# A graph layer on one core: a fill between gathers, a lighter first part, a look-up summed in PSUM and packing operands in PSUM

## The chip, the core and the metric

The kernel runs on one core of a Trainium2 chip. The core has a matrix engine (PE, which writes PSUM), a vector engine (DVE), an activation engine (ACT), a general engine (POOL) and a DMA-issuing engine (SP), each with its own queue of instructions that runs in order; they meet through semaphores. Times are device microseconds of one launch, from the first instruction to the last; lower is better. The time before is 3158.25 us, the median of 3 runs (3149.09 to 3170.76).

## What is computed

One layer for N = 6250 nodes with D = 256 features and 206,250 directed edges (`src`, `dst`). Its first half sums two branches over the layer-normalised input; its second half is a mixture of 8 experts with the two best per node.

```
xn = layernorm(x)
# branch 1: graph attention, 4 heads (gnn)
h = xn @ W                        # 64 features
el, er = h @ Wl.T, h @ Wr.T       # 4 scores each
e = exp(leaky_relu(el[src] + er[dst], 0.2))
w = e / rowsum(e over edges of src)
out_h = elu(segment_sum(w_h * h[dst], src) + b)     # 4 x 64
# branch 2: linear attention over all nodes, 4 heads of 32 (mix), with rmsnorms
q, k, v = split(rmsnorm(xn) @ w_qkv)
k = softmax over the nodes;  context = k v^T;  out = rmsnorm(q context @ w_out + b) + xn
x = x + branch1 + branch2
# experts
t = layernorm(x); top 2 of 8 by router
x = x + t + sum_e combine_e * (gelu(t @ w1_e + b1_e) @ w2_e + b2_e)
```

## The kernel before

Nodes are cut into 49 tiles of 128 (`NT`), edges into 1612 columns of 128 (`EC`).

**First part.** `project(t0, n)` takes four node tiles at a time: it loads x, takes the statistics, normalises (`xn`, L310, on DVE), transposes on PE, multiplies by one joined weight matrix and copies the parts of the PSUM result away: q, k and v with a scale, the row of `table` that the edges gather (4 scores, 64 features and a one, `tab`), and `el`. A running maximum of k (`kmax`) goes along. After each project() three calls of `sort_batch` follow, each over 32 columns of edges: a one-hot of the source's pair of tiles (`ob`, L365), counts on PE (`n_ps`), a scan (`inc`), the number of edges ahead (`before`, L380), ranks through two matmuls (`r_ps`, with the triangular matrix `tri` and `ones16`), and a matmul that puts each edge into its cell of `grid`. Then `context()` subtracts the maximum from k (L468, on DVE), takes Exp and sums k v^T.

**Middle.** A loop runs over the 49 node tiles. For each tile b there are 35 columns of 128 edges. `pack(q)` orders the edges of the pair of tiles 2q and 2q+1: one-hots `ohc` (L858) and `ohp` (L870), products `rc` (L865), matmuls into `s_ps` (L875), and from it the indices `dst_x` (L884, clamped in L886). `gather` then issues 35 indirect DMAs on POOL per tile (L906), each of 128 rows of `table`, into tiles `xe` of 7 columns, of which there are 8: a tile needs five, so the gathers can run 1.6 tiles ahead at most. `look(b, k)` fetches el of each edge's source: one-hots `oh` (L919), transposes, matmuls `e_ps` (L939) in two halves, each with a reduce into `er` (L943). `weights` lines up `er` with the edge columns (`z`, L960 to L964), adds the gathered scores (five adds `z<-z,xe`, L967, one for each xe tile), takes the leaky maximum and Exp (`ew`) and copies it to PSUM (`ew_s`, L972). `sums(k)`, k = 0 to 3, weighs the one-hots (`ohw`, L980) and accumulates 45 matmuls into `a_ps` (L987); it is the last reader of xe.

Between the four steps of a tile stand pieces of other work: `look(b + 1, k)`, at k = 1 of every even tile `pack` of the next pair, and one piece of the second branch's attention or of the experts (`finish_steps`: h_ps L731, Gelu into hT L739, y_ps L747, x L751). The order in which each engine gets its instructions is made by the framework's scheduler when the program is built; each engine then keeps to it. POOL's queue in this part holds the gathers alone. A gather waits for the indices, for a free xe and for the gather eight before it.

The PSUM tile `bank` holds `ew_s` and the bias row `gb_s`. At the end a flag tells whether some pair had more edges than fit; only then a slow path runs.

Of the kernel before, what the change touches and what calls it, by code (L numbers as in the profile page):

```python
# [8 lines left out]
F32 = mybir.dt.float32  # L9
# [8 lines left out]
P = 128  # L18
# [17 lines left out]
def tile_gps_layer(  # L36
# [174 lines left out]
    tri = sp.tile([P, P], F16, name="tri")  # L211
    nc.vector.tensor_scalar(tri, iota_f, piota, None, op0=OP.is_gt)
# [3 lines left out]
    starts = sp.tile([NB, BW // CB, CB], F32, name="starts")  # L216
    nc.vector.memset(starts, 1.0)
    nc.vector.memset(starts[:, :, 0:1], 0.0)
# [69 lines left out]
    def project(t0, n):  # L288
# [16 lines left out]
        tab = qw.tile([P, GT, TW], F32, name="tab")  # L305
        nc.gpsimd.memset(tab[:, :, TW - 1:TW], 1.0)  # L306
        for j in range(n):
            t = t0 + j
            xn = qw.tile([P, D], F32, name="xn")
            nc.vector.tensor_scalar(  # L310
                xn, xt[:, j, :], stats[:, t, 0:1], rstd[:, t:t + 1],
                op0=OP.subtract, op1=OP.mult,
            )
            xT_ps = mps.tile([P, DC, P], F32, name="tp")
            for c in range(DC):
                nc.tensor.transpose(xT_ps[:, c, :], xn[:, c * P:(c + 1) * P], ident)
            xT = qw.tile([P, DC, P], F32, name="xT")
            nc.scalar.copy(xT, xT_ps)
            pr = mps.tile([P, PW], F32, name="pr")
            for c in range(DC):  # L320
                nc.tensor.matmul(
                    pr, lhsT=xT[:, c, :], rhs=wcat[:, c, :], start=(c == 0), stop=(c == DC - 1)
                )
            nc.scalar.activation(q_all[:, t, :], pr[:, :HID], AF.Copy, scale=rn[:, j:j + 1])
            nc.scalar.activation(
                kv[:, t, :2 * HID], pr[:, HID:3 * HID], AF.Copy, scale=rn[:, j:j + 1]
            )
            nc.scalar.copy(tab[:, j, :TW - 1], pr[:, O_TAB:O_EL])
            nc.vector.tensor_copy(el[:, t, :], pr[:, O_EL:PW])
            rows = P if t < NT - 1 else last  # L330
            k_t = kv[:rows, t, :HID]
            if t == 0:
                nc.vector.tensor_copy(kmax, k_t)
            else:
                nc.vector.tensor_max(kmax[:rows], kmax[:rows], k_t)
        nc.sync.dma_start(
            out=table[t0 * P:(t0 + n) * P, :].rearrange("(t p) f -> p t f", p=P),
            in_=tab[:, :n, :],
# [9 lines left out]
    def sort_batch(t):  # L348
# [20 lines left out]
        n_ps = sps.tile([NB, BW], F32, name="n_ps")  # L369
        for c in range(w):  # L370
            nc.tensor.matmul(
                n_ps[:, c:c + 1], lhsT=ob[:, c, :], rhs=ones16[:, 0:1], start=True, stop=True
            )
        inc = sw.tile([NB, BW], F32, name="inc")
        nc.vector.tensor_tensor_scan(
            inc[:, :w], flat(starts)[:, :w], n_ps[:, :w], 0.0,
            op0=OP.mult, op1=OP.add,
        )
        before = sw.tile([NB, BW, 2], F16, name="before")
        nc.vector.tensor_tensor(  # L380
            before[:, :w], inc[:, :w, None].to_broadcast([NB, w, 2]),
            n_ps[:, :w, None].to_broadcast([NB, w, 2]), op=OP.subtract,
        )
        if w == BW:
            nc.scalar.copy(ntot[:, bs], inc[:NQ].rearrange("q (b c) -> q b c", c=CB)[:, :, CB - 1])
        else:
            for b, e in enumerate(ends):
                nc.scalar.copy(ntot[:, bs][:, b:b + 1], inc[:NQ, e - 1:e])
        ahead = sw.tile([NB, BW, NB], F16, name="ahead", bufs=1)
        nc.vector.tensor_tensor(  # L390
            pairs(ahead[:, :w]), two(before[:, :w], NB // 2), row(delta, NB // 2), op=OP.mult
# [3 lines left out]
        for i, a in enumerate(range(0, w, BB)):  # L395
            z = min(w, a + BB)
            part = r_ps[:, i, :(z - a) * NB]
            nc.tensor.matmul(part, lhsT=tri, rhs=flat(ob[:, a:z]), start=True, stop=False)
            nc.tensor.matmul(
                part, lhsT=ones16[:NB, :], rhs=flat(ahead[:, a:z]), start=False, stop=True  # L400
            )
# [9 lines left out]
        rank = sw.tile([P, BW], F16, name="rank")  # L411
        with nc.allow_low_precision("one summand of each sum is not zero"):
            nc.vector.tensor_reduce(rank[:, :w], r16[:, :w], axis=AX.X, op=OP.add)
        rank2 = sw.tile([P, BW, 2], F16, name="rank2")
        nc.vector.tensor_copy(rank2[:, :w], rank[:, :w, None].to_broadcast([P, w, 2]))
# [25 lines left out]
    def context():  # L441
        km_ps = mps.tile([HID, P], F32, name="tp")
# [23 lines left out]
        for t0, n in groups:  # L466
            kk = kv[:, t0:t0 + n, :HID]
            nc.vector.tensor_sub(kk, kk, krow[:, None, :].to_broadcast([P, n, HID]))  # L468
# [333 lines left out]
    yps = gx.enter_context(tc.tile_pool(name="yp", bufs=2, space=PSUM))  # L802

# [3 lines left out]
    gb_s = bank[:, 512 - FO:]  # L807
# [7 lines left out]
    def pack(q):  # L815
# [8 lines left out]
        for u in range(U):  # L824
# [6 lines left out]
            total = pe.tile([P, S, NBT], F32, name="e_ps")  # L831
# [21 lines left out]
        iota_2 = pairs(iota_h)[:, None]  # L853
        s_ps = pl.tile([P, 2, U * CW], F32, name="s_ps")
        for t0 in range(0, NBT, PB):
# [8 lines left out]
            for i in range(2):  # L864
                nc.vector.tensor_tensor(  # L865
                    pairs(rc[:, :m, i, :]), pairs(ohc[:, :m]),
                    twos(grid[:, q, t0:t0 + m, i, :], U * CW // 2), op=OP.mult,
# [31 lines left out]

    def gather(dst_x):  # L900
        xes = []
        for k in range(CPT // EB):
            xe = gw.tile([P, EB, TW], F32, name="xe", bufs=8)
            for j in range(EB):
                c = k * EB + j
                nc.gpsimd.indirect_dma_start(  # L906
# [4 lines left out]
                )  # L911
# [3 lines left out]
    def look(b, k):  # L915

        if k == 0:
# [3 lines left out]
                pairs(iota_b[:, :SN])[:, None].to_broadcast([P, GC * S, SN // 2, 2]),  # L921
# [3 lines left out]
            seen[b] = oh, gw.tile([P, GC, S, H], F32, name="er")  # L925
        elif k < 3:
            oh, er = seen[b]
# [9 lines left out]
            e_ps = pe.tile([P, gh, S, 3, H], F32, name="e_ps")  # L937
            for g in range(gh):
                nc.tensor.matmul(  # L939
                    e_ps[:, g].rearrange("p s i h -> p (s i h)"), lhsT=ohT[:, g, :],  # L940
                    rhs=elw[:, b].rearrange("p s i h -> p (s i h)"), start=True, stop=True,
                )
            nc.vector.tensor_reduce(  # L943
                er[:, g0:g0 + gh].rearrange("p g s h -> p (g s) h"),
                e_ps.rearrange("p g s i h -> p (g s) h i"), axis=AX.X, op=OP.add,
            )

    def weights(xes, er):
        z = gw.tile([P, CW, H], F32, name="z")

        def of(q0, n, a, m):

            zq = z[:, q0 * CS:(q0 + n) * CS].rearrange("p (s j) h -> p s j h", j=CS)
            return zq[:, :, a:a + m]

        def er_of(q0, n, a, m):
            return er[:, a:a + m, q0:q0 + n].rearrange("p g s h -> p s g h")

        more = GC - 1 - CS
        nc.vector.tensor_copy(of(0, S, 0, CS), er_of(0, S, 1, CS))  # L960
        nc.vector.tensor_copy(z[:, CPT - more:CPT], er[:, GC - more:, S - 1])
        head, tail = of(1, S - 1, 0, more), of(0, S - 1, CS - 1, 1)
        nc.vector.tensor_add(head, head, er_of(0, S - 1, GC - more, more))
        nc.vector.tensor_add(tail, tail, er_of(1, S - 1, 0, 1))  # L964
# [3 lines left out]
        zz = z[:, :CPT]  # L968
        nc.vector.scalar_tensor_tensor(zz, zz, 0.2, zz, op0=OP.mult, op1=OP.max)
        ew = gw.tile([P, CPT, H], F32, name="ew")  # L970
        nc.scalar.activation(ew, zz, AF.Exp)
# [40 lines left out]
    for t0, n in blocks:  # L1012
        x2 = gw.tile([P, GT, D], F32, name="x2", bufs=3)
        for j in range(n):
            b = t0 + j
            xes, _ = ready.pop(b)
            oh, er = seen.pop(b)
            weights(xes, er)
# [159 lines left out]
```

## Time and profile before

| | |
|---|---|
| median of the runs | 3158.25 us (3149.09 to 3170.76, 3 runs) |
| the profiled execution | 3989.86 us, span 3988.1 us |
| granted PE clock in it, mean | 0.717 |
| gathers | 1715, 965 ns each on POOL |
| first gather starts | 491.59 us |
| DMA engines, mean | 26 GB/s moved |

The profiled execution is a fourth longer than the runs without a profile, so shares of its span are not shares of the median. Three lines to learn the page's form (instruction group, shapes, count, then busy time and mean in ns, then idle time before and what ended it):

```profile
L870 DVE TENSOR_TENSOR ohp<-to,iota_h 128x2048 f16<-128x2048 f16 x150 | 182.9, 1220 | 24.6 <-remote 16.4 <-PE s_ps L875 4.4 <-ACT to L851 3.8
L943 DVE TENSOR_REDUCE er<-e_ps 128x96 f32<-128x288 f32 x98 | 44.1, 450 | 102.5 <-PE a_ps L987 42.1 <-PE e_ps L939 30.1 <-remote 20.5
masks.py:197 POOL MEMSET ident<- 128x128 f32 x1 | 0.2, 204 | 0.3 <-POOLq L1158 0.3
```

The last one is a memset of 128 elements per partition on POOL, at the program's start.

### The profile page before, as it was taken

How to read it: one execution, taken by the hardware profiler on the slowest of the kernel's cores; microseconds unless marked ns; L12 is line 12 of the kernel's file. 1: busy time of each engine (PE TensorE's matmuls, PEld its weight loads, DVE VectorE, ACT ScalarE, POOL GpSimd, SP SyncE). 2: the span in 40 equal slices, each digit the busy share in tenths (PEclk: the TensorE clock that was granted, in tenths of full speed). 3: DMA queues.
4: the chain of work that ended last, by engine and by line, in shares of the span. 5: the costliest groups of instructions: out<-in, count | busy, mean ns of one | idle time of the engine just before them, and what ended most of it. 6: DMA issues, size and time to landing. Idle time of an engine off the chain costs nothing.

```text
span 3988.1 us, 40348 instructions
## 1 busy us (share of the span) xinstructions
PE 2343.3 (59%) x15298; PEld 1728.2 (43%) x15298; DVE 2045.5 (51%) x4719; ACT 681.1 (17%) x1365; POOL 1666.2 (42%) x1753
## 2 busy tenths in 40 slices
PE   6787633354546666656766573573674654655758
PEld 3444423333334544444544352452453443443546
DVE  8888843456445445534625543553453445255353
ACT  3333201111111211211211110110110101101113
POOL 1000076544654454463454545436345444545430
PEclk8776556666667877776868686686786776776879
DMA  1001012111211111110111101101011011111110
GB/s 57 28 21 17 13 26 45 29 38 43 46 47 48 27 19 23 21 35 14 26 19 23 25 17 26 22 14 33 16 21 28 18 23 21 21 21 25 19 20 9
DMA packets 106684, 103.98 MB, mean 26 GB/s; under 512 B 42726, under 2 KB 78788, under 8 KB 106484
## 3 DMA queue, kind: packets, MB, share of 16 engines
q0 software_dynamic: 54880, 60.70, 9.0%
q1 hardware_dynamic: 49908, 39.75, 3.5%
q8 instruction: 122, 2.00, 0.2%
q10 hardware_dynamic: 1696, 0.89, 0.1%
q14 instruction: 78, 0.64, 0.1%
HBM read 86.57 MB, written 14.65 MB: 25 GB/s over the span
## 4 chain that ended last, share of the span: by engine, by line
another core or an unknown queue 30%; PE 26%; DVE 19%; issue 5%; ACT 3%; POOL 1%; DMA 0%; DVEq 0%; ACTq 0%; POOLq 0%
PE y_ps L747 7%; PE a_ps L987 7%; PE h_ps L731 7%; DVE rc L865 4%; DVE ohp L870 4%; DVE ohc L858 2%; DVE ohw L980 2%; PE s_ps L875 1%; PE y_ps L722 1%; POOL xe L906 1%; PE y_ps L671 1%; PE t_ps L932 1%; PE y_ps L559 1%; ACT ohT L936 1%
## 5 line engine op out<-in xcount | busy, mean ns | idle before, releaser
L906 POOL DMA_INDIRECT xe<-table,dst_x x1715 | 1654.9, 965 | 1901.0 <-issue 767.3
L987 PE MATMUL a_ps<-ohw,xe 128*65 128x128 f32 x4410 | 693.8, 316 | 295.5 <-issue 171.5
L987 PEld LDWEIGHTS a_ps<-ohw,xe 128*65 128x65 f32 x4410 | 614.6, 165 | 392.3 <-issue 229.9
L980 DVE TENSOR_TENSOR ohw<-oh,bank 128x1280 f32<-128x1280 bf16 x196 | 322.6, 1649 | 631.6 <-remote 524.3
L731 PE MATMUL h_ps<-tokT,w1s 128*128 128x512 f32 (+2 forms) x896 | 438.9, 609 | 176.0 <-ACT hT L739 173.3
L747 PE MATMUL y_ps<-w2s,hT 128*128 128x256 f32 x1568 | 434.9, 420 | 73.6 <-DVE x L751 44.1
L747 PEld LDWEIGHTS y_ps<-w2s,hT 128*128 128x128 f32 x1568 | 323.5, 213 | 196.2 <-issue 94.1
L751 DVE SCALAR_TENSOR_TENSOR x<-y_ps,comb,x 128x256 f32<-128x256 f32 x392 | 186.6, 481 | 379.8 <-PE y_ps L747 198.3
L875 PE MATMUL s_ps<-rc,ohp 128*128 128x144 f16 x2525 | 241.3, 264 | 164.9 <-DVE rc L865 156.4
L875 PEld LDWEIGHTS <-ohp 128*128 128x128 f16 x2525 | 219.2, 116 | 216.8 <-issue 127.5
L731 PEld LDWEIGHTS h_ps<-tokT,w1s 128*128 128x128 f32 x896 | 166.3, 210 | 291.8 <-ACT hT L739 198.5
L739 ACT ACTIVATE hT<-h_ps,b1s 128x512 f32<-128x512 f32 (+2 forms) x224 | 142.0, 634 | 828.3 <-PE h_ps L731 379.7
L865 DVE TENSOR_TENSOR rc<-ohc,grid 128x1152 f16<-128x1152 f16 (+1 forms) x350 | 229.1, 693 | 5.2 <-remote 5.2
L870 DVE TENSOR_TENSOR ohp<-to,iota_h 128x2048 f16<-128x2048 f16 (+1 forms) x175 | 195.1, 1115 | 24.6 <-remote 16.4
L722 PE MATMUL y_ps<-b2s,cTs 8*128 8x256 f32 x98 | 53.3, 640 | 208.9 <-issue 107.9
L936 ACT COPY ohT<-t_ps 128x768 bf16<-128x768 bf16 x98 | 78.1, 797 | 334.1 <-remote 144.7
L939 PE MATMUL e_ps<-elw,ohT 128*128 128x48 bf16 x588 | 39.9, 199 | 157.5 <-ACT ohT L936 84.5
L858 DVE TENSOR_TENSOR ohc<-to,iota_h 128x1152 f16<-128x1152 f16 (+1 forms) x175 | 121.3, 694 | 8.8 <-ACT to L851 8.8
L722 PEld LDWEIGHTS y_ps<-b2s,cTs 8*128 8x128 f32 x98 | 21.9, 276 | 230.2 <-issue 122.6
L932 PE MATMUL t_ps<-identb,oh 128*128 128x128 bf16 x588 | 68.6, 269 | 86.7 <-DVE oh L919 79.0
L306 POOL MEMSET tab<- 128x4 f32 x13 | 1.3, 108 | 282.0 <-DMA table<-tab 282.0
L723 DVE TENSOR_TENSOR x<-x,y_ps 128x256 f32<-128x256 f32 x49 | 20.5, 421 | 191.6 <-remote 83.9
(261 smaller groups left out, 2748.6 us busy)
## 6 DMA issues: line engine op xcount, KB each, us to landing
xe<-table,dst_x POOLq DMA_INDIRECT x1715
xt<-in_x_dram SPq DMA_DIRECT2D x24, 512.0 KB
base_y<-xt SPq DMA_DIRECT2D x12, 512.0 KB
yt<-base_y SPq DMA_DIRECT2D x11, 512.0 KB
out_dram<-x SPq DMA_DIRECT2D x11, 512.0 KB
w1s<-in_L_ffn_w_dram SPq DMA_DIRECT2D x8, 256.0 KB
w2s<-in_L_ffn_w_dram SPq DMA_DIRECT2D x8, 256.0 KB
table<-tab SPq DMA_DIRECT2D x12, 138.0 KB
```

The source lines that it names most:

```text
L731: nc.tensor.matmul(h_ps[:, :w], lhsT=w1s[:, e, c, f * P:(f + 1) * P], rhs=held["tokT"][:, c, :w], start=(c == 0), stop=(c == DC - 1),)
L739: nc.scalar.activation(held[e][:, f, :w], h_ps[:, :w], AF.Gelu, bias=b1s[:, k:k + 1])
L747: nc.tensor.matmul(y_ps, lhsT=held[e][:, f, j * P:(j + 1) * P], rhs=w2s[:, e, f, :], start=(f == 0), stop=(f == FC - 1),)
L751: nc.vector.scalar_tensor_tensor(x2[:, j, :], y_ps, held["comb"][:, j, e:e + 1], x2[:, j, :], op0=OP.mult, op1=OP.add,)
L858: nc.vector.tensor_tensor(pairs(ohc[:, :m]), twos(to[:, 0, t0:t0 + m], U * CW // 2), iota_2[:, :, :U * CW // 2].to_broadcast([P, m, U * CW ...
L865: nc.vector.tensor_tensor(pairs(rc[:, :m, i, :]), pairs(ohc[:, :m]), twos(grid[:, q, t0:t0 + m, i, :], U * CW // 2), op=OP.mult,)
L870: nc.vector.tensor_tensor(pairs(ohp[:, :m]), twos(to[:, 1, t0:t0 + m], P // 2), iota_2.to_broadcast([P, m, P // 2, 2]), op=OP.is_equal,)
L875: nc.tensor.matmul(flat(s_ps), lhsT=ohp[:, t - t0, :], rhs=flat(rc[:, t - t0]), start=(t == 0), stop=(t == NBT - 1),)
L906: nc.gpsimd.indirect_dma_start(out=xe[:, j, :], out_offset=None, in_=table, in_offset=bass.IndirectOffsetOnAxis(ap=dst_x[:, c:c + 1], axis=0),
L936: nc.scalar.copy(ohT, t_ps)
L980: nc.vector.tensor_tensor(ohw[:, :n], oh[:, g0:g1, i, None, :].to_broadcast([P, n, H, SN]), ew_s[:, c0:c0 + n, :, None].to_broadcast([P, n ...
L987: nc.tensor.matmul(a_ps[:, i].rearrange("f h n -> f (h n)"), lhsT=xes[c // EB][:, c % EB, H:], rhs=ohw[:, c - c0].rearrange("p h n -> p (h ...
```

## The change

It has four parts.

1. In `gather`, a memset of 128x128 f32 (one of 16 slots of `pause`) stands on POOL in front of each indirect DMA, and dependencies without a semaphore fix the order memset, gather, memset, gather.
2. The first part: `xn` goes from DVE to ACT (with `shift` = -mean * rstd as bias), `el` is copied with `tab` on ACT and split off on POOL, `kmax` becomes one reduce at the start of context(), the subtraction of the maximum goes to POOL, the rank's copy to ACT. In sort_batch the count matmul gives two columns, count and zero, so that a scan over 64 elements yields the inclusive count without a `before`; where `tri` was, `upto` (minus one where column <= row) stands, and the rank's reduce is halved by a fold first.
3. The look-up: the 12 matmuls of a tile add into one PSUM tile `e_ps` by edge column, after one matmul with zeros; a single reduce in `weights` replaces two reduces and four copies and adds. `total` in pack() moves from the PSUM pool `pe` to `pt`.
4. Packing: `iota_h`, `iota_b` and the pair's slice of `grid` are copied into `bank` as f32 words and read from PSUM as 16-bit operands by ohc, ohp, rc and oh.

```
@@ project
-        tab = qw.tile([P, GT, TW], F32, name="tab")
-        nc.gpsimd.memset(tab[:, :, TW - 1:TW], 1.0)
+        shift = qw.tile([P, GT], F32, name="shift")
+        nc.vector.scalar_tensor_tensor(
+            shift[:, :n], stats[:, t0:t0 + n, 0], -1.0, rs, op0=OP.mult, op1=OP.mult
+        )
+        tab = qw.tile([P, GT, TW - 1 + H], F32, name="tab")
...
-            nc.vector.tensor_scalar(
-                xn, xt[:, j, :], stats[:, t, 0:1], rstd[:, t:t + 1],
-                op0=OP.subtract, op1=OP.mult,
+            nc.scalar.activation(
+                xn, xt[:, j, :], AF.Identity, bias=shift[:, j:j + 1], scale=rstd[:, t:t + 1]
             )
...
-            nc.scalar.copy(tab[:, j, :TW - 1], pr[:, O_TAB:O_EL])
-            nc.vector.tensor_copy(el[:, t, :], pr[:, O_EL:PW])
-            rows = P if t < NT - 1 else last
-            k_t = kv[:rows, t, :HID]
-            if t == 0:
-                nc.vector.tensor_copy(kmax, k_t)
-            else:
-                nc.vector.tensor_max(kmax[:rows], kmax[:rows], k_t)
+            nc.scalar.copy(tab[:, j, :], pr[:, O_TAB:PW])
+        nc.gpsimd.tensor_copy(el[:, t0:t0 + n, :], tab[:, :n, TW - 1:])
+        nc.gpsimd.memset(tab[:, :n, TW - 1:TW], 1.0)
@@ sort_batch
-        n_ps = sps.tile([NB, BW], F32, name="n_ps")
+        n_ps = sps.tile([NB, BW, 2], F32, name="n_ps")
         for c in range(w):
             nc.tensor.matmul(
-                n_ps[:, c:c + 1], lhsT=ob[:, c, :], rhs=ones16[:, 0:1], start=True, stop=True
-            )
-        inc = sw.tile([NB, BW], F32, name="inc")
+                n_ps[:, c, :], lhsT=ob[:, c, :], rhs=one_none, start=True, stop=True
+            )
+        inc = sw.tile([NB, BW, 2], F16, name="inc")
         nc.vector.tensor_tensor_scan(
-            inc[:, :w], flat(starts)[:, :w], n_ps[:, :w], 0.0,
-            op0=OP.mult, op1=OP.add,
-        )
-        before = sw.tile([NB, BW, 2], F16, name="before")
-        nc.vector.tensor_tensor(
-            before[:, :w], inc[:, :w, None].to_broadcast([NB, w, 2]),
-            n_ps[:, :w, None].to_broadcast([NB, w, 2]), op=OP.subtract,
+            flat(inc[:, :w]), starts.rearrange("q b c two -> q (b c two)")[:, :2 * w],
+            flat(n_ps[:, :w]), 0.0, op0=OP.mult, op1=OP.add,
         )
...
-            nc.tensor.matmul(part, lhsT=tri, rhs=flat(ob[:, a:z]), start=True, stop=False)
+            nc.tensor.matmul(part, lhsT=upto, rhs=flat(ob[:, a:z]), start=True, stop=False)
...
+        fold = NB // 4 * 2
+        nc.vector.tensor_tensor(
+            r16[:, :w, :fold], r16[:, :w, :fold], r16[:, :w, NB - fold:], op=OP.add
+        )
-            nc.vector.tensor_reduce(rank[:, :w], r16[:, :w], axis=AX.X, op=OP.add)
+            nc.vector.tensor_reduce(
+                rank[:, :w], r16[:, :w, :NB - fold], axis=AX.X, op=OP.add
+            )
-        nc.vector.tensor_copy(rank2[:, :w], rank[:, :w, None].to_broadcast([P, w, 2]))
+        nc.scalar.copy(rank2[:, :w], rank[:, :w, None].to_broadcast([P, w, 2]))
@@ context
+        nc.vector.tensor_reduce(
+            kmax, kv[:, :NT - 1, :HID].rearrange("p t d -> p d t"), axis=AX.X, op=OP.max
+        )
+        nc.vector.tensor_max(kmax[:last], kmax[:last], kv[:last, NT - 1, :HID])
...
-            nc.vector.tensor_sub(kk, kk, krow[:, None, :].to_broadcast([P, n, HID]))
+            nc.gpsimd.tensor_sub(kk, kk, krow[:, None, :].to_broadcast([P, n, HID]))
@@ middle: bank
+    none = gw.tile([1, (1 + CPT) * 3 * H], BF16, name="none", bufs=1)
+    nc.vector.memset(none, 0.0)
...
-    gb_s = bank[:, 512 - FO:]
+    gb_s = bank[:, CPT * H:CPT * H + FO]
+    words = CPT * H + FO
+    iota_p = bank[:, words:words + P // 2]
+    iota_q = bank[:, words + P // 2:words + (P + SN) // 2]
+    words += (P + SN) // 2
+    edges = bank[:, words:words + 2 * NBT]
+    nc.vector.tensor_copy(iota_p, iota_h.bitcast(F32))
+    nc.vector.tensor_copy(iota_q, iota_b[:, :SN].bitcast(F32))
+    iota_p, iota_q = iota_p.bitcast(F16), iota_q.bitcast(BF16)
@@ pack
-            total = pe.tile([P, S, NBT], F32, name="e_ps")
+            total = pt.tile([P, S, NBT], F32, name="t_ps")
...
+        nc.vector.tensor_copy(
+            edges, grid[:, q].rearrange("p t i two -> p (t i two)").bitcast(F32)
+        )
+        edges_q = edges.bitcast(F16).rearrange("p (t i two) -> p t i two", i=2, two=2)
-        iota_2 = pairs(iota_h)[:, None]
+        iota_2 = pairs(iota_p)[:, None]
...
-                    twos(grid[:, q, t0:t0 + m, i, :], U * CW // 2), op=OP.mult,
+                    twos(edges_q[:, t0:t0 + m, i, :], U * CW // 2), op=OP.mult,
@@ gather
+    rows = []
+    pause = gw.tile([P, 16, P], F32, name="pause", bufs=1)
+
+    def behind(ins, by=mybir.DependencyClass.NoSync):
+        if rows:
+            tc.add_manual_dep(
+                ins.ins, rows[-1].ins.name,
+                mybir.DependencyInfo(by, mybir.DependencyReason.DATA),
+            )
+        rows.append(ins)
...
-                nc.gpsimd.indirect_dma_start(
+                slot = len(rows) // 2 % 16
+                behind(nc.gpsimd.memset(pause[:, slot], 0.0))
+                behind(nc.gpsimd.indirect_dma_start(
...
@@ look
-            seen[b] = oh, gw.tile([P, GC, S, H], F32, name="er")
+            seen[b] = oh, pe.tile([P, 1 + CPT, 3, H], F32, name="e_ps")
...
-            e_ps = pe.tile([P, gh, S, 3, H], F32, name="e_ps")
+            if k == 1:
+                nc.tensor.matmul(
+                    e_ps.rearrange("p c i h -> p (c i h)"), lhsT=identb[0:1, :], rhs=none,
+                    start=True, stop=False,
+                )
             for g in range(gh):
                 nc.tensor.matmul(
-                    e_ps[:, g].rearrange("p s i h -> p (s i h)"), lhsT=ohT[:, g, :],
-                    rhs=elw[:, b].rearrange("p s i h -> p (s i h)"), start=True, stop=True,
-                )
-            nc.vector.tensor_reduce(
-                er[:, g0:g0 + gh].rearrange("p g s h -> p (g s) h"),
-                e_ps.rearrange("p g s i h -> p (g s) h i"), axis=AX.X, op=OP.add,
-            )
+                    e_ps[:, g0 + g::CS][:, :S].rearrange("p s i h -> p s (i h)"),
+                    lhsT=ohT[:, g, :],
+                    rhs=elw[:, b].rearrange("p s i h -> p s (i h)"),
+                    start=False, stop=(g0 + g == GC - 1),
+                )
@@ weights
-        nc.vector.tensor_copy(of(0, S, 0, CS), er_of(0, S, 1, CS))
-        nc.vector.tensor_copy(z[:, CPT - more:CPT], er[:, GC - more:, S - 1])
-        head, tail = of(1, S - 1, 0, more), of(0, S - 1, CS - 1, 1)
-        nc.vector.tensor_add(head, head, er_of(0, S - 1, GC - more, more))
-        nc.vector.tensor_add(tail, tail, er_of(1, S - 1, 0, 1))
+        nc.vector.tensor_reduce(
+            z, e_ps[:, 1:].rearrange("p c i h -> p c h i"), axis=AX.X, op=OP.add
+        )
```

## The prediction

> **What bounds the kernel now.** I read the page first: span, busy shares, slices, the head of the chain.
>
> ```profile
> span 3988.1 us, 40348 instructions
> PE 2343.3 (59%) x15298; PEld 1728.2 (43%) x15298; DVE 2045.5 (51%) x4719; ACT 681.1 (17%) x1365; POOL 1666.2 (42%) x1753
> POOL 1000076544654454463454545436345444545430
> another core or an unknown queue 30%; PE 26%; DVE 19%; issue 5%; ACT 3%; POOL 1%; DMA 0%; DVEq 0%; ACTq 0%; POOLq 0%
> L906 POOL DMA_INDIRECT xe<-table,dst_x x1715 | 1654.9, 965 | 1901.0 <-issue 767.3
> ```
>
> No engine is full. The POOL digits show three stretches: a first part without gathers, a long middle with them, a short tail. The windows give each its own numbers (columns: us, then busy time and count of PE, PEld, DVE, ACT, POOL, then granted clock, DMA share, GB/s):
>
> ```profile
> 0.00:491.00 491.00, 352.47 (x3954) 218.51 (x3954) 427.48 (x973) 153.15 (x475) 11.36 (x38) 0.72 0.11 25
> 491.00:3860.00 3369.00, 1882.36 (x10851) 1434.21 (x10851) 1571.93 (x3602) 482.46 (x808) 1654.80 (x1715) 0.71 0.13 27
> 3860.00:3988.00 128.00, 108.51 (x493) 75.50 (x493) 46.12 (x146) 45.45 (x82) 0.08 (x1) 0.88 0.05 8
> ```
>
> The first part is DVE's (427 of 491 us, 87%), the tail PE's. In the middle POOL sets the rhythm; its timeline (start, length, in brackets the idle time before and what ended it):
>
> ```profile
> 1784.76 0.94 POOL L906 DMA_INDIRECT xe<-table,dst_x  x1 [0.30 <-issue]
> 1836.39 1.65 POOL L906 DMA_INDIRECT xe<-table,dst_x  x1 [50.69 <-issue]
> ...
> 2980.01 0.95 POOL L906 DMA_INDIRECT xe<-table,dst_x  x1 [28.80 <-PE y_ps L747]
> 2981.26 0.94 POOL L906 DMA_INDIRECT xe<-table,dst_x  x1 [0.30 <-issue]
> 2982.51 0.94 POOL L906 DMA_INDIRECT xe<-table,dst_x  x1 [0.30 <-issue]
> ```
>
> In a burst a gather starts every 1.25 us (0.94 and 0.30). 1715 of them are 2139 us of the middle's 3369; in the other 1230 us POOL waits. The long waits, like the 28.80, come before every even tile: POOL wants `dst_x` of the next pair of tiles, and pack() on DVE is not done (its `dst_x` clamp, L886, began at 2979.08). Shorter ones are for xe buffers (350.6 us released by a_ps L987).
>
> Why is pack late? In a burst PE slows down: from 3000 to 3018 us it starts a matmul every 1.2 to 2.6 us, its wait put to "issue", where 0.11 us is usual at full clock; DVE waits for it.
>
> ```profile
> 3011.23 0.20 PE L939 MATMUL e_ps<-elw,ohT 128*128 128x48 bf16 x1 [1.91 <-issue]
> 3012.61 0.20 PE L939 MATMUL e_ps<-elw,ohT 128*128 128x48 bf16 x1 [1.19 <-issue]
> 3022.43 1.75 DVE L980 TENSOR_TENSOR ohw<-oh,bank 128x1536 f32<-128x1536 bf16 x1 [26.37 <-remote]
> ```
>
> First part and tail, without gathers, have no such stall. The profiled execution took 3989.86 us, the median of the runs is 3158.25: 832 us less, while the stalls are some 30% of 3988. So I take most of the stall to be the profile's own. On the median my ledger is 491 + 2139 + 128 = 2758 and some 400 us of POOL waiting, 17 us for each of the 24 pairs. That split is an estimate; no row shows the unprofiled run.
>
> **The change, part by part.**
>
> *Fill between gathers.* 1715 memsets of 128x128 f32. A memset of that size (masks.py:197, ident) took 204 ns, so 350 us on POOL's queue if nothing overlaps, 0 if it fits into the 0.30 us gap. Below nothing only if the spacing frees PE in the bursts, which I weigh as a rival. The full price stands by its row; but the 1.25 us rhythm may itself be a little slow under the profile. For both together I take the middle of 2139 and 2489: 2314 us. Each xe tile also comes 7 x 0.2 us later; z adds and a_ps wait for it.
>
> *First part.* DVE loses xn 19.7, kmax 13.3, before 9.9, rank2 9.0, kv subtract 8.0, el 7.8, tri 3.1: 70.8 us. It gains shift (13 x 0.17 = 2.2), one kmax reduce of 6144 elements (at L413's 1003 ns for 832: 7), 32 more scan elements x 50 (1.7); rank by fold and half-size reduce is 0.35 + 0.60 against 1.00 us, -2.6 in all. Net -63 us. ACT takes xn (49 x 0.42, by L562) and rank2 (50 x 0.19), +30 us on 153 of 491: covered, though DVE now waits for ACT's rank2 with only rv to do meanwhile. POOL takes the 13 kv subtracts: 0.67 us each by DVE's row, 1.3 at twice that; POOL is idle there (its waits for table stores are 282 us). The table stores now wait for POOL's el copy and memset instead of ACT; nobody waits for them before the first gather. First gather at about 441: -50, ends 0 and -63.
>
> *Look-up in PSUM.* Off DVE: 98 reduces of 450 ns (44 us) and four z operations (0.23, 0.16, 0.19, 0.17 us) x 49 (37 us). On: 49 reduces of 420 elements, 0.59 us by scaling L943 (29 us). -52 us over 49 tiles, but in front of the z adds, which wait for gathers: I take 0. PE gets 49 zero-matmuls of 432 columns (0.43 us by L832's 0.405: 21 us), covered by a PE that is 56% busy.
>
> *Packing operands in PSUM.* 25 copies of edges (0.36 us by L972: 9 us). The large question is the rate. L870 (ohp, 2048 f16 elements, both operands in SBUF) took 1220 ns, two per cycle. No row here reads f16 from PSUM. In f32 a PSUM operand costs nothing: L838 with one 568 ns, L839 without 561. The Trainium skill (VectorE: DVE Perf Modes, "The perf-mode tier table") speaks against this edit: tensor_tensor with any PSUM operand runs at one element per cycle. Its Vector Engine (DVE) Microarchitecture Reference ("5.1 Performance modes") asks for 16-bit unit-step operands but not SBUF in that mode. By the first, 34,744 elements per pack at 0.52 ns more are 18 us x 25 = 452 us, and oh 49 x 0.8 = 39; by the second nothing. I take the second and keep the first as a rival.
>
> *What moves: DVE's order.* This decides my forecast. I compared the built instruction order. Before, in 22 of the 24 packs that run inside the tile loop the five adds of gathered rows for the next tile (z<-z,xe, L967) stand behind all 14 rc multiplies. After, in 14 of 24 all five adds stand ahead of at least 12 of the 14 rc (packs 1 to 7, 10, 13, 15, 17, 19, 21, 23); in 7 more ahead of the last few operations. DVE runs in order, so there pack waits for the odd tile's last gather to land; then come ohc, ohp, rc and the index arithmetic; only then has POOL indices. Queued behind the waiting add are also ohw of k=2 and 3 (now behind all rc), so a_ps and the xe buffers it frees. Price: landing 2 us (tile 0: gathers end at 539, `ew` is copied at 543.4, between them 2.4 us of adds, Exp and its table), then from the first ohc to dst_x 23 us (2956.08 to 2979.27), two ohw 3.5, some routing operations 2: about 30 us of idle POOL per gated pair, 14 x 30 = 420 us. The trace of before has this case twice: packs 6 and 10 stand behind four and three of the adds, and POOL waited 38.0 and 50.7 us there, against 23 to 30 elsewhere late in the run. For the ten other pairs I take 5 us (50), for buffers 3 us x 24 (72).
>
> **Sum.** 441 + 2314 + 420 + 50 + 72 + tail 128 = 3425; rounded 3430, +8.6% on 3158. In a profiled execution the same edits act on 3988, where pack already ran after the bursts; there I expect a smaller change, -5% to +10%.
>
> **Rivals.**
> 1. *The bursts' stalls are real and the fill loosens them* (faster). For it: 30% of the chain. Against: PE trickles record by record, and the median lacks 832 us of it. Place: PE between 7 gathers into a burst and its end. Price: at best the 400 us of POOL waiting fall to 200 and the fill hides half: 441 + 2314 + 200 + 128 = 3083; it decides if the gated packs cost less than the 17 us per pair paid now. 13%.
> 2. *The fill hides in the gap* and only the gate remains: 2139 for 2314, 3250. 17%.
> 3. *One element per cycle from PSUM*: 18 us more in front of each dst_x, on the path in the gated pairs and half of the rest: 19 x 18 = 342, 3770. 6%.
> 4. *It cancels*: the gate binds only where POOL waits already, the first part pays for the fill: 3158 - 50 + 40, within 1%. 8%.
>
> **How the numbers follow.** My case has 56%, with 3300 to 3590 by the two ends of the fill. The range 3120 to 3590 leaves out rival 1 and rival 3. 1% is about what a measurement of this kernel can tell from no change (its three runs lie 0.7% apart). Faster 0.13; within 1% 0.08; slower 0.56 + 0.17 + 0.06 = 0.79.
>
> **What would show it.** After: the gather's period in bursts (1.25 if hidden, 1.45 if not); POOL's idle before even tiles (30 us or more in the listed pairs, released by DVE); ohp at 1220 ns or 2280; the first gather near 441; PE's "issue" trickle in bursts gone or not. I am wrong if the median falls below 3127, which means that the stalls exist outside the profile, or if the gated pairs wait no longer than the others.

## The result, and the profile after

The changed kernel takes 3508.68 us (median of 4 runs, 3507.48 to 3511.68) beside 3156.69 us for the kernel before (4 runs, 3149.09 to 3170.76): ratio 1.1111, 95% interval 1.1071 to 1.1151. It is slower by 11%, on a chip of this kind. Another kind turned up in the experiments, and there the answer has the other sign.

First the page of the changed kernel: span, engines, and the groups that answer to those shown before.

```profile
span 3506.6 us, 42107 instructions
PE 2212.4 (63%) x15347; PEld 1630.4 (46%) x15347; DVE 1992.4 (57%) x4307; ACT 722.9 (21%) x1471; POOL 2082.0 (59%) x3494
L945 POOL DMA_INDIRECT xe<-table,dst_x x1715 | 1655.0, 965 | 934.6 <-PE a_ps L1016 621.6
L944 POOL MEMSET pause<- 128x128 f32 x1715 | 382.5, 223 | 60.5 <-PE g_ps L433 59.5
L997 DVE TENSOR_TENSOR z<-z,xe 128x28 f32<-128x28 f32 x245 | 44.4, 191 | 845.4 <-DMA xe<-table,dst_x 801.7
L895 DVE TENSOR_TENSOR ohp<-to,bank 128x2048 f16<-128x2048 f16 (+1 forms) x175 | 194.9, 1114 | 0.0
```

No engine is full. POOL is idle for 934.6 us in front of its gathers (some 285 of it is the usual gap of 0.17 us; the ledger below has the real waits), and DVE waits 801.7 us in its adds of gathered rows for those same gathers: the two wait for each other in turn. ohp reads f16 from PSUM at 1114 ns in the mean.

The three stretches of the run, cut some 20 us before the first gather and 4 us before the last one (columns as in the prediction):

```profile
0.00:434.00 434.00, 326.77 (x3869) 198.43 (x3869) 380.46 (x756) 190.56 (x580) 48.72 (x65) 0.76 0.13 29
434.00:3380.00 2946.00, 1782.55 (x11003) 1360.35 (x11004) 1566.84 (x3415) 487.04 (x812) 2029.22 (x3423) 0.74 0.15 31
3380.00:3507.00 127.00, 103.04 (x477) 71.60 (x475) 45.05 (x139) 45.30 (x79) 4.11 (x7) 0.88 0.07 9
```

Now one gated pack, on DVE's timeline (start, length, engine and line, then in brackets the idle time before), and POOL's first gather after it:

```profile
1273.27 0.19 DVE L997 TENSOR_TENSOR z<-z,xe 128x28 f32<-128x28 f32 x1 [1.67 <-DMA xe<-table,dst_x]
1273.37 0.26 DVE L867 TENSOR_TENSOR to_i<-inc 128x101 int32<-128x101 f32 x1
1283.04 0.19 DVE L997 TENSOR_TENSOR z<-z,xe 128x28 f32<-128x28 f32 x1 [9.41 <-DMA xe<-table,dst_x]
...
1283.42 0.20 DVE L868 TENSOR_SCALAR to_i<-to_i 128x101 int32<-128x101 int32 x1
...
1284.16 0.75 DVE L883 TENSOR_TENSOR ohc<-to,bank 128x1152 f16<-128x1152 f16 x1
...
1309.43 0.20 DVE L911 TENSOR_SCALAR dst_x<-dst_x 128x72 int32<-128x72 int32 x1
```

```profile
1310.37 0.95 POOL L945 DMA_INDIRECT xe<-table,dst_x  x1 [29.72 <-PE a_ps L1016]
1311.32 0.22 POOL L944 MEMSET pause<- 128x128 f32 x1
```

The fifth add stands in the queue between two steps of pack's index arithmetic. It waits 9.41 us, until tile 13's last rows have landed; only then come all of ohc, rc and ohp, and dst_x 26 us later. POOL starts 0.7 us after dst_x, after 29.72 us of idling. The trace names a_ps as what ended that wait, because the wait is for several semaphores; what came last is the dst_x clamp, whose end lies directly before the gather.

From POOL's timeline I made one ledger for every kernel. *First*: start of gather 0. *Rhythm*: the time from the first to the last gather without the waits. *Waits*: idle time of POOL beyond the usual gap, in front of even tiles (where a new pair begins) and elsewhere. *Tail*: from the last gather to the end. "Stalls" marks runs on chips on which the kernel before takes some 3960 us (see below).

| kernel, us | first | rhythm | waits, even tiles | other waits | tail | span |
|---|---|---|---|---|---|---|
| changed | 455 | 2310 | 607 | 12 | 122 | 3507 |
| e1 no fill | 455 | 2165 | 618 | 13 | 127 | 3379 |
| e2 pack first | 455 | 2317 | 321 | 5 | 129 | 3227 |
| e3 operands in SBUF | 452 | 2396 | 251 | 11 | 128 | 3237 |
| e4 before + fill | 494 | 2394 | 185 | 9 | 128 | 3210 |
| e7 before, stalls | 491 | 2181 | 681 | 487 | 128 | 3967 |
| e5 before + first part, stalls | 453 | 2181 | 641 | 495 | 127 | 3898 |
| e6 no fill, pack first, stalls | 453 | 2158 | 811 | 373 | 128 | 3923 |
| e10 changed, stalls | 457 | 2308 | 737 | 215 | 133 | 3850 |
| e9 fill, pack earlier, stalls | 455 | 2310 | 29 | 897 | 129 | 3820 |

### The profile page after: what moved, and what is told of

The parts are those of the page before. It is cut to its first block, busy times and chain, and to the rows that moved or that the text cites. A ratio compares the mean times of both kernels' runs of the same rounds, so it can differ in the third digit from the quotient of the medians.

```text
span 3506.6 us, 42107 instructions
## 1 busy us (share of the span) xinstructions
PE 2212.4 (63%) x15347; PEld 1630.4 (46%) x15347; DVE 1992.4 (57%) x4307; ACT 722.9 (21%) x1471; POOL 2082.0 (59%) x3494
## 5 line engine op out<-in xcount | busy, mean ns | idle before, releaser
L945 POOL DMA_INDIRECT xe<-table,dst_x x1715 | 1655.0, 965 | 934.6 <-PE a_ps L1016 621.6
L1016 PE MATMUL a_ps<-ohw,xe 128*65 128x128 f32 x4410 | 611.5, 299 | 298.5 <-issue 230.1
L1016 PEld LDWEIGHTS a_ps<-ohw,xe 128*65 128x65 f32 x4410 | 563.2, 155 | 338.0 <-issue 245.9
L997 DVE TENSOR_TENSOR z<-z,xe 128x28 f32<-128x28 f32 x245 | 44.4, 191 | 845.4 <-DMA xe<-table,dst_x 801.7
L756 PE MATMUL y_ps<-w2s,hT 128*128 128x256 f32 x1568 | 405.2, 395 | 127.4 <-DVE x L760 107.0
L944 POOL MEMSET pause<- 128x128 f32 x1715 | 382.5, 223 | 60.5 <-PE g_ps L433 59.5
L890 DVE TENSOR_TENSOR rc<-ohc,bank 128x1152 f16<-128x1152 f16 (+1 forms) x350 | 227.6, 692 | 1.9 <-DVE z L997 0.2
L895 DVE TENSOR_TENSOR ohp<-to,bank 128x2048 f16<-128x2048 f16 (+1 forms) x175 | 194.9, 1114 | 0.0
L883 DVE TENSOR_TENSOR ohc<-to,bank 128x1152 f16<-128x1152 f16 (+1 forms) x175 | 121.1, 692 | 0.0
L427 DVE TENSOR_TENSOR ohp<-rank,iota_h 128x4096 f16<-128x4096 f16 (+1 forms) x51 | 115.7, 2270 | 2.8 <-ACT rank L420 2.8
L325 PE MATMUL pr<-wcat,xT 128*128 128x456 f32 x196 | 106.3, 670 | 5.8 <-ACT xT L322 4.3
```

The costliest lines, as they stand in the source:

```text
L756: nc.tensor.matmul(y_ps, lhsT=held[e][:, f, j * P:(j + 1) * P], rhs=w2s[:, e, f, :], start=(f == 0), stop=(f == FC - 1),)
L883: nc.vector.tensor_tensor(pairs(ohc[:, :m]), twos(to[:, 0, t0:t0 + m], U * CW // 2), iota_2[:, :, :U * CW // 2].to_broadcast([P, m, U * CW ...
L890: nc.vector.tensor_tensor(pairs(rc[:, :m, i, :]), pairs(ohc[:, :m]), twos(edges_q[:, t0:t0 + m, i, :], U * CW // 2), op=OP.mult,)
L895: nc.vector.tensor_tensor(pairs(ohp[:, :m]), twos(to[:, 1, t0:t0 + m], P // 2), iota_2.to_broadcast([P, m, P // 2, 2]), op=OP.is_equal,)
L944: behind(nc.gpsimd.memset(pause[:, slot], 0.0))
L945: behind(nc.gpsimd.indirect_dma_start(out=xe[:, j, :], out_offset=None, in_=table, in_offset=bass.IndirectOffsetOnAxis(ap=dst_x[:, c:c + 1 ...
```

## The experiments

### On the chip without stalls

**e1, no fill.**

```
-                behind(nc.gpsimd.memset(pause[:, slot], 0.0))
```

> The changed kernel without the 1715 memsets; 12 instead of 14 packs stand behind the next tile's adds. My theory now (the fill's net price is 0.09 us a gather; a gated pair pays it on 70 gathers, a free pair only on the 35 of its even tile, because its pack is late anyhow): 14 x 6.3 + 10 x 3.2 = 120 us less, 3390 us. The prediction's own term (2314 for 2139) says 175 less, 3333. Rival, the fill is the whole slowdown: about 3157 - 37 = 3120. For the profile: if the fill alone takes the profile's inflation away, this kernel's profiled execution is again some hundreds of us above its median, with matmuls 1.2 us and more apart in the bursts.

Measured: 3381.65 us (3380.26 to 3383.16), 1.0734 [1.07, 1.0768] of before (3152.42 on this chip, 0.1% from the 3156.69 beside the changed kernel). The fill costs 127 us in this order; theory 120. The rhythm falls by 145 us, 0.085 us for each gather: of a memset's 0.223 us the rest fits into the gap. Of the 145 us, 12 come back as longer waits and 5 in the tail. The whole slowdown is not the fill's: 229 us are left. The last sentence of the expectation failed: without the fill, the profiled execution is still as long as the others (3381.0).

**e2, pack first.** The adds of gathered rows get an order-only dependency on the last dst_x clamp.

```
-        nc.vector.tensor_scalar_min(dst_x, dst_x, NPAD - 1)
+        packed.append(nc.vector.tensor_scalar_min(dst_x, dst_x, NPAD - 1))
...
-            nc.vector.tensor_add(zk, zk, xe[:, :, :H])
+            add = nc.vector.tensor_add(zk, zk, xe[:, :, :H])
+            tc.add_manual_dep(
+                add.ins, packed[-1].ins.name,
+                mybir.DependencyInfo(
+                    mybir.DependencyClass.NoSync, mybir.DependencyReason.DATA
+                ),
+            )
```

> The changed kernel, with the adds of gathered rows ordered behind the dst_x clamp of the last pack, so that no pack is gated; fill and all else stay. By the prediction's prices (30 us for a gated pair, 5 for a free one) 14 x 25 = 350 us less: 3160. By the waits in the changed kernel's own trace (28 to 32 us for a gated pair, 18 to 20 for a free one) only 14 x 11 = 154 less: 3355, with 18 us of POOL idle before every even tile. Rival, the order costs nothing: 3508.

Measured: 3229.98 us (3228.59 to 3235.84), 1.0258 [1.0224, 1.0292]. The order alone is worth 279 us, more than any other part of the change. In the ledger all of it is the wait before even tiles, 607 to 321. By pairs, the 14 listed in the prediction fall from 29.1 us each (25.2 to 32.0) to 9.7; the other ten from 20.0 to 18.6. Both my numbers were off: 350 by the prediction's prices, 154 by "28 to 32 against 18 to 20". One of the ten, pair 8, waits 29.6 us although no add stands ahead of its pack; the other nine wait 17.7 to 20.1. A gated pair without its gate does not fall to the level of the others, but below, because its pack starts earlier: pair 7's first ohc comes 3.7 us after the odd tile's last gather in the changed kernel, and 8.5 us before it in e2.

**e3, operands in SBUF.**

```
-        iota_2 = pairs(iota_p)[:, None]
+        iota_2 = pairs(iota_h)[:, None]
...
-                    twos(edges_q[:, t0:t0 + m, i, :], U * CW // 2), op=OP.mult,
+                    twos(grid[:, q, t0:t0 + m, i, :], U * CW // 2), op=OP.mult,
...
-                pairs(iota_q)[:, None].to_broadcast([P, GC * S, SN // 2, 2]),
+                pairs(iota_b[:, :SN])[:, None].to_broadcast([P, GC * S, SN // 2, 2]),
```

> The changed kernel with iota_h, iota_b and grid read from SBUF as before, no copies into bank. The built order has then 3 gated packs for 14. Theory (the PSUM operands cost nothing in themselves, they only changed the scheduler's order): as the run with pack first, 11 x 11 = 120 less, 3390; by the prediction's prices 11 x 25 = 275 less, 3233. Rival, operands in PSUM gain time or cost it by themselves: this run and the one with pack first lie more than 60 us apart.

Measured: 3235.46 us (3234.17 to 3238.84), 1.0268 [1.0235, 1.03]: 5 us from the run with pack first. So it is this part of the change, the operands in PSUM with the copies into `bank` that go with them, that led the scheduler to the gating order (how it did was not looked into); undone alone, with fill, first part and look-up kept, it gives back 273 of the 279 us. But "they cost nothing in themselves" hides two effects that cancel. The gathers take 1014 ns in the mean here and 969 with operands in PSUM, and the rhythm is 2396 for 2317: the PSUM operands make POOL 79 us faster. First this run's kind of gather beside pack, in the kernel before with fill (e4), where the operands are also in SBUF; then the same stretch of work with operands in PSUM (e2):

```profile
1305.33 0.22 POOL L919 MEMSET pause<- 128x128 f32 x1
1305.72 0.95 POOL L920 DMA_INDIRECT xe<-table,dst_x  x1 [0.17 <-issue]
1306.67 0.22 POOL L919 MEMSET pause<- 128x128 f32 x1
1307.05 1.42 POOL L920 DMA_INDIRECT xe<-table,dst_x  x1 [0.17 <-issue]
```

```profile
1260.18 0.95 POOL L947 DMA_INDIRECT xe<-table,dst_x  x1 [0.17 <-issue]
1261.13 0.22 POOL L946 MEMSET pause<- 128x128 f32 x1
1261.52 0.95 POOL L947 DMA_INDIRECT xe<-table,dst_x  x1 [0.17 <-issue]
```

While ohc, ohp and rc run, gathers of 0.95 us become 1.42 us in the first and not in the second; over all 1715, 166 are longer than 1.3 us in e4 and 28 in e2. In the mean, gathers that lie beside ohp take 1343 ns in e4 (116 of them) and 951 in e2 (79), beside rc 1262 and 956, beside ohc only 1030 and 951; beside ohw, which has one operand in PSUM in both kernels, 957 and 954. So the instruction beside a gather makes the difference, and not the kernel as a whole. The DVE instructions themselves keep their times (rc 692 ns in e3, 689 in e2). The Trainium skill (SBUF — State Buffer, "Who interferes with whom") says that a DVE instruction with two SBUF inputs contends with a GpSimd instruction that reads SBUF, and one with at most one SBUF input, outside the modes that use both ports, does not; these rows agree.

**e4, the kernel before with the fill alone** (the memset and its order, as in the change).

> The kernel before with the fill and its fixed order alone; the order on DVE is that of before (no pack gated). Theory: 24 free pairs x 35 gathers x 0.09 = 77 us more, 3235. The prediction's term: 175 more, 3332. Rival, the fill hides in the gap: 3157. Profile: if the stalls of the kernel before are the profile's own and come from gathers issued without a pause, this kernel's profiled execution lies within 1% of its median and its burst matmuls are no longer 1.2 us apart.

Measured: 3213.08 us (3211.55 to 3214.78), 1.02 [1.0167, 1.0232], so 61 us more; theory 77. Here, where no pack is gated, most of the fill's 145 us seems to be paid out of waits that POOL would have had anyway; the kernel before has no trace without stalls that could show them. In the ledger 11 of the 24 pairs wait less than 3 us; in eight of these pack's first scan runs ahead of the copy of the even tile's `ew_s`.

### On chips with stalls

**e5, e6, e7, e8** ran on another chip. There the kernel before takes 3965.72 us (median of 19 runs, all but one of them between 3940.8 and 3985.36), 813 us more than on the first. The totals expected of e5, e6 and e8 were meant for a chip without stalls; here only the difference from the kernel before can be read.

> The kernel before, nothing changed, profiled once more. If its profiled execution is always long (3990 us, matmuls 1.2 us and more apart in bursts), it is again above 3900. If that was one odd execution, this one lies within 1% of 3152, and its trace shows what the median run does: about 17 us of POOL idle before each even tile by the prediction's ledger (400 us in 24 pairs).

e7 is the kernel before, unchanged: its profiled execution takes 3968.97 us, as long as the other runs on its chip. One group of its page, ohw on DVE, against the same group of e1 (the last numbers are DVE's idle time before it, and what ended most of that; "remote" is a release to which the trace shows no instruction):

```profile
L980 DVE TENSOR_TENSOR ohw<-oh,bank 128x1280 f32<-128x1280 bf16 x196 | 322.5, 1649 | 608.0 <-remote 454.9
```

```profile
L1006 DVE TENSOR_TENSOR ohw<-oh,bank 128x1280 f32<-128x1280 bf16 x196 | 323.0, 1648 | 78.0 <-PE a_ps L1013 75.9
```

And matmuls of a_ps within a burst, PE's timeline, first e7, then e1 (x20 are 20 matmuls in a row):

```profile
2427.14 0.37 PE L987 MATMUL a_ps<-ohw,xe 128*65 128x128 f32 x1 [0.98 <-issue]
2428.55 0.37 PE L987 MATMUL a_ps<-ohw,xe 128*65 128x128 f32 x1 [1.04 <-issue]
2431.34 0.37 PE L987 MATMUL a_ps<-ohw,xe 128*65 128x128 f32 x1 [2.42 <-issue]
```

```profile
629.80 2.35 PE L1013 MATMUL a_ps<-ohw,xe 128*65 128x128 f32 x20
```

POOL gathers at the same pace in both (1.27 and 1.26 us each), but in e7 PE starts one matmul in 1.4 to 2.8 us, and in e1 twenty in 2.35 us. The stall does not come from the profiler, since the profiled executions of e1 to e4 have none and are as short as their other runs. It goes with the chip; each chip was used in one session only, so that chip and session cannot be told apart. The long "remote" idle time before ohw is also in the 3990 us execution shown before the change (524.3 us): that one was most likely taken on such a chip, while the 3158 us median came from the other kind. A lower granted clock does not explain the stall. Before the first gather the clock is 0.72 in e7 and 0.71 in e4 (the kernel before with the fill, no stalls), and the first gather comes at 491 and 494 us; within bursts it is 0.58 and 0.78, a quarter less, while PE's rate in the table under e10 falls to less than a quarter (0.89 for 4.04).

**e5, first part alone** (the kernel before with the new project, sort_batch and context).

> The kernel before with the lighter first part alone (the middle and its order as before, but one more pack, the fourth, behind two adds). The first gather starts 37 us earlier (455 for 492), one more gated pair costs 11: 3152 - 37 + 11 = 3126. The prediction's term: 3152 - 50 = 3102. Rival, the first part's gain is lost again in the middle: 3152.

Measured 3917.18 us (14 runs), 0.9904 [0.9868, 0.9939]. In the ledger the first gather comes 38 us earlier (453 for 491), and the gain is kept.

**e6, no fill and pack first** (both edits of e1 and e2).

> The changed kernel without the fill and with no pack gated: first part, look-up in PSUM and operands in PSUM are what is left of the change. Theory (gate and fill are the whole loss): the free pairs of the run with pack first pay the fill on the 35 gathers of the even tile alone, 24 x 3.2 = 77 less than its 3230: 3153. If all 70 gathers of a pair count, 154 less: 3076. Rival, look-up and PSUM operands cost time of their own on the path: above 3170.

Measured 3923.5 us, 0.9909 [0.9874, 0.9945]. What it takes on a chip without stalls was not seen. Here nothing beyond what the first part's 38 us explain comes through.

**e8, pack one tile earlier, no fill.** The gathers leave pack() and stay where they were.

```
+    packed = {}
+
+    def fetch(q):
+        for b in range(q * U, min(q * U + U, NT)):
+            idx, loc = packed.pop(b)
+            ready[b] = (gather(idx), loc)
...
-                if k == 1 and b % U == 0 and b + U < NT:
-                    pack(b // U + 1)
+                if k == 1 and b % U == 0 and b + U < NT:
+                    fetch(b // U + 1)
+                if k == 1 and b % U == 1 and b + U + 1 < NT:
+                    pack(b // U + 2)
```

> The changed kernel without the fill, pack of a pair one tile earlier (in the odd tile before the pair's predecessor ends), gathers where they were; no pack is gated. Theory (the chain from the even tile's last gather to dst_x, some 60 us against the odd tile's 44 us of gathers, is what POOL waits for in every pair): POOL no longer waits for indices, only for buffers; 455 + 2139 + 122 = 2716 at the least, with 100 us of buffer waits 2820. Rival, buffers (a_ps behind ohw) or PE end the wait at the same place: 3100 and above.

Measured 4027.78 us, 1.0187 [1.0151, 1.0223]. The wait before even tiles is gone (77 us), but 1209 us appear elsewhere, before odd tiles and inside tiles. PE starts 0.68 matmuls a us in bursts and 4.06 in POOL's pauses. My reading, which no run isolates, is that PE's work needs those pauses, wherever they stand.

**e9, the same with the fill.**

> The changed kernel with its fill, and pack one tile earlier. The kernel before has now taken 3152 us on one chip and 3966 on another, with the stalls in bursts on the second only, so this run is read beside the kernel before on its own chip. Theory (POOL then waits for buffers alone): 455 + 1715 x 1.335 + 122 = 2867 at the least, about 2950 with 80 us of buffer waits. If the fill takes the stalls away, that holds on either kind of chip; if it does not, then on the chip with stalls this kernel is near the 4028 of its form without the fill. Rival on a chip without stalls: buffers or PE end the wait at the same place, 3180 and above.

It came on a third chip, again with stalls (before 3956.55): 3855.96 us, 0.9729 [0.9676, 0.9782]. Against e8 (other chip, before within 0.3%) the fill gains 172 us. It loosens the stalls without removing them: 1.69 matmuls a us in bursts for 0.68 in e8.

**e10, the changed kernel again.**

> The changed kernel, nothing changed. On a chip where the kernel before takes about 3155, again 3508. On a chip where it takes about 3960 (stalls in bursts): theory, the stalls already push pack and the sums behind the bursts there, so the gate costs little and the fill gives the other engines air: 3700 to 3900, faster than before by 2 to 7%. Rival, the 352 us come on top of the stalls: 4310.

On a fourth chip with stalls (before 3967.66, 10 runs): 3864.36 us (3851.48 to 3872.14), 0.9757 [0.9723, 0.9791]. The change that costs 11% on one chip gains 2.4% on this one. By the ledger against e7: first gather -35, rhythm +127, even tiles +56, other waits -272, tail +5. The count of matmuls fits the last large term (bursts: at least 14 gathers with no gap above 1 us, counted from 14 us after their start; pauses: POOL idle for more than 5 us):

| matmuls started per us | in bursts | in pauses |
|---|---|---|
| e7 before, stalls | 0.89 | 4.51 |
| e6 no fill, pack first, stalls | 0.72 | 4.17 |
| e11 the same, operands in SBUF, stalls | 1.19 | 4.53 |
| e10 changed, stalls | 1.55 | 4.64 |
| e1 no fill, no stalls | 3.00 | 4.83 |
| changed, no stalls | 2.82 | 4.75 |
| e4 before + fill, no stalls | 4.04 | 5.46 |

With stalls and without a fill, PE starts about one matmul for each gather (0.7 to 1.2, at 0.8 gathers a us). With a fill of 0.22 us in every 1.35 it is 1.55. Without stalls the fill does not show in PE's rate: 3.00 without it and 2.82 with it, in nearly the same order.

**e11, first part and look-up only**: no fill, operands in SBUF, pack first.

> The changed kernel without the fill, with the operands in SBUF and no pack gated: of the change the first part and the look-up in PSUM are left. On a chip without stalls: theory, the first part's 38 us come through and the look-up is nothing: 3152 - 38 = 3114. If the look-up's 52 us of DVE time a run also shorten the chain to dst_x, 3070; if it costs, above 3152. On a chip with stalls: against the same with operands in PSUM (3923 beside 3966 for before, 0.991) no difference beyond 1%.

On the chip of e10: 3939.41 us, 0.9939 [0.991, 0.9969], within the expected 1% of e6's 0.9909. The look-up in PSUM neither gains nor costs anything that can be told from this; the first part alone, on another such chip, had 0.9904.

**e12, as e8 with 12 xe buffers for 8.**

```
-            xe = gw.tile([P, EB, TW], F32, name="xe", bufs=8)
+            xe = gw.tile([P, EB, TW], F32, name="xe", bufs=12)
```

> The changed kernel without the fill, pack one tile earlier, and 12 xe buffers for 8, so that POOL waits neither for indices nor for the buffers of the tile before. On a chip without stalls: theory (POOL's waits are all that lies above its rhythm), 455 + 2165 + 125 = 2745, with 50 us of waits 2795; rival, PE and DVE cannot follow and end the run themselves, 2950 or more. On a chip with stalls the kernel with 8 buffers took 4028 beside 3966: if those waits were for buffers, 3700 to 3850; if the gathers hold up the other engines whatever POOL's order is, 3900 to 4030.

On a fifth chip, with stalls again (before 3948.71): 4050.66 us, 1.0237 [1.0167, 1.0306]. POOL now waits 17 us before even tiles and 1273 elsewhere. The time is above both ranges that were expected here, 20 us over the one for gathers that hold up the other engines whatever POOL's order is. More room moves POOL's waits and does not shorten the run; PE's rate stays at 0.79 matmuls a us in bursts and 4.08 in pauses.

## Why the prediction was right, and where it was not

The forecast was 3430 us, slower; 3508.68 was measured. Two things were luck. The kernel before and the changed kernel were both measured without stalls, where the sum holds; on a chip with stalls the sign is the other one (e10). And the total is off by no more than 81 us because errors offset each other: the ten other pairs are 150 too low, the other waits 60 too high. Its terms against the trace of the changed kernel:

| term | predicted | measured |
|---|---|---|
| first gather | 441 | 455 |
| gathers with fill | 2314 | 2310 |
| 14 gated pairs | 420 | 407 |
| ten other pairs | 50 | 200 |
| other waits | 72 | 12 |
| tail | 128 | 122 |
| sum | 3425 | 3506 |

*Gate.* Right in place and in size: 14 x 29.1 us for 14 x 30. Net of what the same pairs wait without the gate it costs 279 us (e2), where the prediction's prices, with 5 us for a free pair, say 350. e2 shows that the order causes it, and e3 which edit caused the order.

*Ten other pairs: the term that failed.* I took 5 us for each; they wait 20.0. Their packs are not behind the odd tile's adds (or only with their last operations), but they begin late all the same, behind the even tile's adds, part of its sums and a piece of the experts. For tile 18 the scan starts at 1517, 23 us after the copy of tile 16's `ew_s`; in between DVE works on two ohw and on x, and PE on a_ps, h_ps and y_ps, which stand ahead of the matmul that the scan waits for. Then dst_x comes at 1552, 35 us later, while the odd tile's gathers ended at 1535. In pair 8, the one that waits 29.6 us, the scan starts 44 us after `ew`, again behind x of the experts. The prediction had written down 17 us a pair for the kernel before, and then dropped it from the sum for the changed kernel without a reason.

*Fill.* The middle between "hidden" and "full price" was the right place (2310 for 2314), though not for both reasons given: of a memset's 0.223 us, 0.085 reach the rhythm, but the 1.25 us period of before is not the profile's own (e1, without stalls, has it too). The two ends of the fill would give 3250 to 3600; the 3300 to 3590 written there is a slip. And the rhythm is not the price: in the order of before 61 us of it reach the time (e4), in the gated order 127 (e1).

*First part.* 37 us for 50. DVE is busy for 401 us up to the first gather, 27 less than the 428 before. The kmax reduce took 11.0 us for the 7 assumed, the scan gained 3.5 for 1.7, and about 6 us of the attention's work on q_all (10.7 for 4.7) now stand ahead of the first gather. The 3.1 us of tri were not won either: delta, now first in its place, takes 3.0 us for 0.2. These come to some 15 of the 36 us between the 63 forecast and the 27 measured; the rest is spread over small differences and overlaps.

*Operands in PSUM.* The step kept its rate: ohp's mean is 1114 ns with PSUM (L895 above) and 1114 in e3 with SBUF:

```profile
L883 DVE TENSOR_TENSOR ohp<-to,iota_h 128x2048 f16<-128x2048 f16 (+1 forms) x175 | 195.0, 1114 | 1.0 <-PE s_ps L888 0.6
```

Rival 3 is out, and the rule on PSUM operands that was weighed there does not hold for these f16 operations. The step missed what the edit does for POOL: 79 us of rhythm.

*"Most of the stall is the profile's own": wrong.* On e7's chip the other runs are as long as the profiled one, and in e1 the profiled execution (3381.00) is as short as the others. The stalls are real, on four of the five chips that the experiments ran on. My sum from the median came out all the same, because that median was from a chip without them; no trace of the kernel before without stalls shows whether the 400 us of waits in it are right. On the chips with stalls rival 1 is what happens: the fill loosens the bursts, and the sum of the change is faster (0.9757), though not by what rival 1 said. The change expected there, -5% to +10% on 3988, holds with -2.4%.

What adds up to +352 on the chip without stalls: first part -38 (first gather, and e5), fill +61 in the old order (e4), gate +279 (e2). The rest, 50 us, lies between e4 and e2 net of the first part: the rhythm is 77 shorter there and the waits before even tiles 136 longer, since in e2 every pack starts behind the even tile's `ew_s` and in e4 nine start ahead of it. That split is read from the ledger; no run isolates it.

Open: what makes a chip stall was not found, only that it sits between gathers on POOL and the start of instructions on PE. No version faster than before was seen on a chip without stalls; e6, e8, e11 and e12 were meant for one and ran on others. With stalls, e9 (0.9729) and the changed kernel (0.9757) are the fastest, with intervals that overlap.

## What to carry to other kernels

When an edit changes where operands lie or what depends on what, compare the built order of each in-order engine before anything else: here moving operands to PSUM sped up the gathers and yet lost 279 us, because waits for data were put ahead of the work that feeds the next gathers. Put an explicit order between such a producer and such waits. Before reading a stall as the profiler's, compare its time with the other runs on the same chip; and time an edit that spaces out gathers on more than one chip.

## What was not expected of the hardware

- The same program takes 3142 to 3171 us in the runs of the result and of e1 to e4, and 3939 to 3991 us, one run apart, on four other chips. The gather rhythm is nearly the same (2165 us in e1, 2181 in e7); what differs in the traces is PE's rate while gathers are issued (0.7 to 1.7 against 2.8 to 4.0 matmuls a us).
- On a chip with stalls a POOL memset of 0.22 us between gathers raises that rate from 0.7 to 1.2 matmuls a us to 1.55. On a chip without, it costs 0.085 us a gather, and no gain was seen.
- Gathers beside ohp and rc, f16 operations on DVE, take 1.26 to 1.39 us in the mean when both inputs are in SBUF (e3 and e4), and 0.95 to 0.96 with one input in PSUM (e2).
